# Turning the divided sums behind the product of v, and their product with Wo behind the next slot's sums of v

## The chip, the cores and the metric

The kernel runs on one core of a Trainium2 chip. The metric is the device time of one execution in microseconds; times of different runs are compared by their median. A core has five engines that run side by side, each with its own queue of instructions: TensorE (PE: products and turnings, that is transposes through the array), VectorE (DVE), ScalarE (ACT), GpSimd (POOL), and SyncE (SP), which here issues the transfers. Products land in PSUM, from which DVE or ACT copy them.

## The reference

The input x has 8 sequences of 512 rows of 128 numbers. Two residual blocks follow each other. The first is an attention with 16 heads of width 8, whose weights come from four Newton steps in place of a softmax (here called the stieltjes part):

```python
for _ in range(num_iter):                      # 4
    d = jnp.maximum(lam[..., None] - s, EPS)
    w = jnp.where(mask, d ** (-q), 0.0)
    f = w.sum(-1) - 1.0
    ...
    lam = lam - f / fp
```

The second is a stack of 6 layers, each a windowed attention (16 heads of width 64, windows of 32 rows, each looking at itself and the window before) and a feed forward with a gated gelu, both added to x:

```python
for i in range(DEPTH):                         # 6
    x = attn_layer(shift_tokens(x), Wqkv[i], q_scale[i], k_scale[i], Wo[i]) + x
    x = ffn_layer(shift_tokens(x), ln_g[i], ln_b[i], W1[i], b1[i], W2[i], b2[i]) + x
```

In `attn_layer`, `out = local_attention(q, k, v)` is divided by the softmax's sums, laid side by side over the heads, and `out @ Wo` is the layer's result. The change is about these last steps: divide, turn, multiply with Wo.

## The kernel before

**Units and slots.** The layers run on the sequences as 48 units, one for each layer and sequence. The sequences go in three groups, (0, 1), (2, 3, 4) and (5, 6, 7), and within a group all sequences take a layer before any takes the next. A unit has 16 heads, in 8 pairs; two pairs are a quarter, and one pair is the work of one slot. The main loop runs over `t`, one slot at a time (384 pairs and a few slots more), as a pipeline written out by hand: in slot t it works on pair t, on pair t - 2 and on pair t - 3, and prepares a later quarter.

**The steps of a slot, in the order in which the code issues them.** The names of the tiles are those of the profile.
- `turn` (L733, L738): q and k of pair t are turned on PE into `ptq` and copied by ACT to `qT`, twice.
- `gather` (L787, L795, L796), for pair t - 3: the sums of v, 64 small products into `po`; DVE takes the reciprocal `rs` of the row sums and writes the divided sums `o`.
- `turn_weights` (L776, L777), for pair t - 2: the softmax weights are turned into `pT` and copied by ACT to `prT`.
- `prepare_qk` (L667 and on), for half of a later quarter: two products `m`; DVE multiplies them with tables (`qr`, L672), ACT squares them (`sq`, L678), POOL adds (L682); then sums of squares and scales (L689 to L695). It ends in a call of `gelus`.
- `exponentials` (L769), for pair t - 1, and `gelus`, which runs a waiting gelu between two loads of ACT's tables (L822, L824). `follow` and `marks` keep these ACT instructions in their order.
- `turn_sums` (L804, L808), for pair t - 3: the divided sums `o` are turned on PE into `po` (L804), and ACT copies them to `oT`.
- `weigh` (L752, L757 to L763), for pair t: 64 small products `s`; DVE adds the mask, takes the maximum, POOL subtracts it.
- `prepare_v` (L704, L707): the product `pv`, which ACT copies to `v`; every other slot `spread` then issues the transfers that lay v out by windows.
- `leave` (L812), for pair t - 3: the product of `oT` with Wo, added up over the 8 pairs of a unit in the PSUM tile `acc`. Behind a unit's last pair the sum is added to the sequence's `xT` (L1034), and a feed forward is appended to `parts`.

**The feed forward** is a generator in seven stages (shifted copy, turning `px`, scales, turning `pn`, product `gp` with the gelu's input, product `ap`, product `y`). `further` takes one stage on. It is called once a slot, and three times more in `dense` slots, those that finish pairs of group (0, 1).

**The stieltjes part** is a generator too. `tick(n)` stands between the steps of a slot and advances it by as many of its own steps as the plan for this slot asks. The first two sequences run it alone; for the others it runs beside the layers, and in the last third of the span it is done.

**Order and buffers.** A scheduler puts the instructions of each engine in an order, which follows the order of issue where its own model of the times lets it; on the chip each engine keeps that order. Most PSUM tiles come from one pool of five banks (`bank`, tag "mm": `ptq`, `pT`, `m`, `pv`, the turned sums, the feed forward's and the stieltjes part's). `s` and the sums of v share one buffer (tag "two"), and `acc` has one of its own. The tiles `o2` and `oT2` have one buffer each.

Of the kernel before, what the change touches and what calls it, by code (L numbers as in the profile page):

```python
# [9 lines left out]
F32 = mybir.dt.float32  # L10
BF16 = mybir.dt.bfloat16
AF = mybir.ActivationFunctionType
ALU = mybir.AluOpType
# [3 lines left out]
P = 128  # L17
N = 512
# [32 lines left out]
def tile_kernel(  # L51
# [18 lines left out]
    nc = tc.nc  # L70
# [18 lines left out]
    units = [(l, b) for grp in groups_of for l in range(DEPTH) for b in grp]  # L89
# [10 lines left out]
    ps_c = ctx.enter_context(tc.tile_pool(name="ps_c", bufs=1, space=PSUM))  # L100
# [398 lines left out]
    def bank(shape, name):  # L499
        return ps_a.tile(shape, F32, name=name, tag="mm")  # L500
# [3 lines left out]
    xT = {}  # L504
# [12 lines left out]
    def advance(upto):  # L517
        nonlocal done_steps
        while done_steps < upto:
            next(first, None)  # L520
            done_steps += 1
# [92 lines left out]
    def load_wo(l, hv):  # L614
        wo = wp.tile([P, NPAIR // 2, D], F32, name="wo", tag=f"wo{hv}")
        nc.sync.dma_start(wo, f_wo[l][hv * HC : (hv + 1) * HC, :].rearrange("(c p) d -> p c d", p=P))
        return wo

    def load_tables(l, h):
        tab = wp.tile([P, 2, 4, DHL], F32, name="tab", tag=f"tab{h}")  # L620
        nc.sync.dma_start(tab, tabs[l][:, 2 * h : 2 * h + 2])
        return tab

    def load_ffn_weights(l):
        w1 = wp.tile([P, 2 * DI], F32, name="w1")
        nc.sync.dma_start(w1, f_w1[l])
        w2 = wp.tile([P, NCH, D], F32, name="w2")
        for k, (c0, cn) in enumerate(CH):
            nc.sync.dma_start(w2[:cn, k, :], f_w2[l][c0 : c0 + cn, :])
        return w1, w2  # L630
# [11 lines left out]
    PQ = 2  # L642
# [84 lines left out]
    def turn(a):  # L727
        g, p = a["g"], a["p"]
        a["qT"] = qT = []
        for t in range(2):  # L730
            pt = bank([P, N], "ptq")
            for c in range(NT):
                nc.tensor.transpose(  # L733
                    pt[:, c * P : (c + 1) * P],
                    g["qn"][:, c, t, 2 * p : 2 * p + 2, :].rearrange("p h e -> p (h e)"), ident,
                )
            q = tp.tile([P, N], F32, name=f"qT{t}")
            nc.scalar.copy(q, pt)  # L738
            qT.append(q)
# [31 lines left out]
    def turn_weights(a):  # L771
        pr = a["pr"]
        a["prT"] = prT = tp.tile([P, NT, P], F32, name="prT")
        pT = bank([P, NT, P], "pT2")
        for c in range(NT):
            nc.tensor.transpose(pT[:, c, :], pr[:, c].rearrange("p e k -> p (e k)"), ident)  # L776
        nc.scalar.copy(prT, pT)  # L777

    def gather(a):
        g, p, prT = a["g"], a["p"], a["prT"]  # L780
        po = ps_b.tile([P, 2, N], F32, name="po2", tag="two")
        po = po[:, :, 0 : NT * (DHL + 1)].rearrange("p e (c f) -> p e c f", c=NT)
        for n in range(NQ):
            c, u = n // UB, n % UB
            for e in range(2):
                rows = slice(e * KB, (e + 1) * KB)
                nc.tensor.matmul(  # L787
                    po[u * QB : (u + 1) * QB, e, c, :],
                    lhsT=prT[rows, c, u * QB : (u + 1) * QB],
                    rhs=g["v3"][rows, n, p, :],  # L790
                    start=True, stop=True,
                )
        a["o"] = o = tp.tile([P, NT, 2, DHL], F32, name="o2")
        rs = tp.tile([P, 2, NT], F32, name="rs", bufs=2)
        nc.vector.reciprocal(rs, po[:, :, :, DHL])  # L795
        nc.vector.tensor_tensor(  # L796
            o.rearrange("p c e f -> p e c f"), po[:, :, :, 0:DHL],
            rs.unsqueeze(3).to_broadcast([P, 2, NT, DHL]), ALU.mult,
        )

    def turn_sums(a):
        pt = bank([P, N], "po3")
        for c in range(NT):
            nc.tensor.transpose(  # L804
                pt[:, c * P : (c + 1) * P], a["o"][:, c].rearrange("p e f -> p (e f)"), ident
            )
        a["oT"] = oT = tp.tile([P, N], F32, name="oT2")
        nc.scalar.copy(oT, pt)  # L808

    def leave(a, wo, acc):  # L810
        pp = a["g"]["qt"] * PQ + a["p"]
        nc.tensor.matmul(  # L812
            acc, lhsT=wo[:, pp % (NPAIR // 2), :], rhs=a["oT"],
            start=(pp == 0), stop=(pp == NPAIR - 1),
        )
# [84 lines left out]
    LAG = 2  # L900
    NS = NPAIR
# [3 lines left out]
    wo = {hv: load_wo(l0, hv) for hv in range(2)}  # L905
    tab = [load_tables(l0, h) for h in range(2)]
    w12 = [load_ffn_weights(l0)]
# [19 lines left out]
    def tick(n):  # L927
        if entering:
            next(entering[0], None)
        advance(span[0] + (span[1] - span[0]) * n // TICKS)  # L930

    def further():
        parts[:] = [n for n in parts if next(n, n) is not n]

    def open_quarter(i):
        u, qt = quarters[i]
        if qt == 0 and units[u][0] == 0:
            settle()
        groups.append(begin(u, qt, shifted(units[u][1], ep) if qt == 0 else groups[-1]["xs"]))

    def prepared(g):
        u, qt = g["u"], g["qt"]
        spread(g)
        if u + 1 < len(units) and units[u + 1][0] != units[u][0]:
            if qt % 2:
                wq[qt // 2] = load_qkv(units[u + 1][0], qt // 2)
# [6 lines left out]
        prepare_qk(groups[0], wq[0], tab[h], cs)  # L953
        prepare_v(groups[0], wq[0], cs)
    prepared(groups[0])
    pairs, parts, acc = [], [], None
    slots = len(quarters) * PQ
    end = slots - 3 * NS * DEPTH - NS
    stages = [(0, 5 * STEPS, end, total)]
    if len(groups_of) > 1:  # L960
        n = len(groups_of[0]) * NS * DEPTH + (len(groups_of[1]) - 1) * NS - 8
        g = ready_at[groups_of[1][-1]]
        stages = [(0, 5 * STEPS, n, g), (n, g, end, total)]
    t = -1
    while t < slots + LAG + 1 or parts:
        i, p = t // PQ, t % PQ
        a = done = last = ahead = None
        if 0 <= i < len(quarters):
            a = dict(g=groups[i], p=p)
            pairs.append(a)  # L970
        if LAG <= t < len(pairs) + LAG:
            done = pairs[t - LAG]
        if LAG + 1 <= t < len(pairs) + LAG + 1:
            last = pairs[t - LAG - 1]
        dense = last and units[last["g"]["u"]][1] in groups_of[0] and len(groups_of) > 1
        n0, g0, n1, g1 = next(s for s in stages if t + 2 <= s[2] or s is stages[-1])
        goal = g0 + (g1 - g0) * (t + 2 - n0) // (n1 - n0)
        span[:] = done_steps, max(done_steps, min(goal, total))
        if a:
            turn(a)  # L980
        tick(1)
        if last:
            gather(last)
        tick(2)
        if done:
            turn_weights(done)
        tick(3)

        i, h = (t + 1) // PQ + 1, (t + 1) % PQ
        if i < len(quarters):  # L990
            if h == 0:
                open_quarter(i)
            ahead = groups[i]
            cs = (2 * h, 2 * h + 1)
            prepare_qk(ahead, wq[ahead["qt"] // 2], tab[h], cs)
            u = ahead["u"] + 1
            if ahead["qt"] == NS // PQ - 1 and u < len(units) and units[u][0] != units[u - 1][0]:
                tab[h] = load_tables(units[u][0], h)
        tick(6)
        if dense:  # L1000
            further()
        if 1 <= t < len(pairs) + (0 if a else 1):
            exponentials(pairs[t - 1])
        gelus()
        tick(7)
        if last:
            turn_sums(last)
        if dense:
            further()
        tick(8)  # L1010
        if a:
            weigh(a)
        tick(9)
        if dense:
            further()
        if ahead:
            prepare_v(ahead, wq[ahead["qt"] // 2], cs)
            if h == PQ - 1:
                prepared(ahead)
        tick(10)  # L1020
        further()
        tick(11)
        if last:
            u, qt = last["g"]["u"], last["g"]["qt"]
            l, b = units[u]
            hv = qt // 2
            if last["p"] == 0 and qt == 0:
                acc = ps_c.tile([P, N], F32, name="acc")
            leave(last, wo[hv], acc)
            if last["p"] == PQ - 1:  # L1030
                if qt % 2 and u + 1 < len(units) and units[u + 1][0] != l:
                    wo[hv] = load_wo(units[u + 1][0], hv)
                if qt == NS // PQ - 1:
                    nc.vector.tensor_tensor(xT[b], xT[b], acc, ALU.add)  # L1034
                    parts.append(feed_forward(u, *w12[0]))
        tick(12)
        t += 1
        u = (t + 6) // NS
        if u < len(units):
            need(units[u][1])  # L1040
# [51 lines left out]
```

## Time and profile before

| | |
|---|---|
| median of 3 runs | 4685.11 us (4684.45 to 4686.75) |
| the profiled execution, its time | 4683.56 us |
| its span, first to last instruction | 4681.8 us |
| PE busy | 4029.8 us (86%) |
| DVE busy | 3935.3 us (84%) |
| ACT busy | 3532.1 us (75%) |
| POOL busy | 3177.3 us (68%) |
| mean granted clock of PE | 0.939 |
| L812, product with Wo | 768 instructions, 414.6 us busy |
| L667, products m | 1536 instructions, 759.4 us busy |

Busy time is the time in which the engine worked on an instruction; matmuls overlap, and their ends are modelled, so PE's own pace is better seen from the starts of its instructions. A product in 32-bit floats shows as two instructions. A line of waits names who waited, for whom, for how long in total, how often, and the longest. In a timeline the columns are the start, the time taken, the engine, the line, the operation and its tiles, and, in brackets, the idle time of the engine ahead of it with what ended it.

### The profile page before, as it was taken

To read this page: it belongs to the slowest core of one execution; us is meant where nothing else is said; L and a number is where in the kernel's file an instruction comes from. 1 tells how busy PE (TensorE), PEld (TensorE's weight loads), DVE (VectorE), ACT (ScalarE), POOL (GpSimd) and SP (SyncE) were. 2 spreads that over 40 slices of the span, in tenths; PEclk is the share of its full clock that TensorE was granted. 3 is DMA by queue.
4 is the path that set the end of the run, shared out by engine and by line. 5 is a ranking of instruction groups with operands and counts; after the bars stand their busy time and mean duration, and the time that the engine had idled before them with its cause. 6 is when DMAs were issued, how large, how long until landed. Compare 5 with 4: busy or idle time off the path is not lost.

```text
span 4681.8 us, 165984 instructions
## 1 busy us (share of the span) xinstructions
PE 4029.8 (86%) x68749; PEld 2507.4 (54%) x68749; DVE 3935.3 (84%) x8788; ACT 3532.1 (75%) x6716; POOL 3177.3 (68%) x4081
## 2 busy tenths in 40 slices
PE   4344688887888888898988999998999999999998
PEld 1233455554455544555555555555666666666665
DVE  7878788887888888998998999999787788877785
ACT  7998677777788777888887888888666666666664
POOL 4543666666666666776777767777787777777774
PEclk7667799999999999999999999999999999999999
DMA  1000222222122222232222222222243333333332
GB/s 49 1 1 1 67 59 51 62 55 59 46 66 61 60 53 62 62 72 50 59 67 54 69 54 70 53 59 68 66 102 83 85 90 75 88 79 86 89 75 59
DMA packets 558912, 288.87 MB, mean 62 GB/s; under 512 B 97580, under 2 KB 541264, under 8 KB 558160
## 3 DMA queue, kind: packets, MB, share of 16 engines
q1 hardware_dynamic: 558160, 278.26, 25.4%
q8 instruction: 543, 8.90, 0.8%
q14 instruction: 209, 1.71, 0.1%
HBM read 66.21 MB, written 7.34 MB: 16 GB/s over the span
## 4 chain that ended last, share of the span: by engine, by line
PE 41%; ACT 26%; DVE 22%; POOL 8%; issue 2%; DMA 1%; SPq 1%; ACTq 0%; POOLq 0%; DVEq 0%
PE m L667 8%; ACT d L301 7%; ACT d L309 5%; PE ptq L733 4%; PE pv L704 4%; DVE stw L289 4%; PE acc L812 4%; DVE qr L672 4%; PE po L787 3%; PE s L752 3%; PE pT L776 3%; POOL ns L276 3%; DVE raw L689 3%; ACT sq L678 2%; PE s L263 2%
## 5 line engine op out<-in xcount | busy, mean ns | idle before, releaser
L682 POOL TENSOR_TENSOR qn<-qr 128x512 f32<-128x512 f32 x768 | 970.0, 1280 | 493.6 <-DVE qr L672 440.5
L672 DVE TENSOR_TENSOR qr<-m,tab 128x1024 f32<-128x1024 f32 x768 | 913.5, 1217 | 157.7 <-PE m L667 116.2
L695 POOL TENSOR_TENSOR qn<-qn,ss 128x512 f32<-128x512 f32 x768 | 786.3, 1046 | 299.5 <-ACT ss L692 285.2
L667 PE MATMUL m<-wqkv,xs 128*128 128x512 f32 x1536 | 759.4, 608 | 16.1 <-ACT prT L777 3.7
L678 ACT ACTIVATE sq<-m 128x512 f32<-128x512 f32 x768 | 459.5, 600 | 394.1 <-DVE qr L672 385.1
L301 ACT ACTIVATE d<-ns,lam 128x416 f32<-128x416 f32 (+7 forms) x1024 | 590.4, 625 | 91.6 <-DVE lam L345 71.0
L289 DVE BATCH_NORM_STATS2 stw<-d 128x6 f32<-128x480 f32 (+7 forms) x1024 | 545.8, 563 | 122.7 <-ACT d L309 120.3
L276 POOL TENSOR_TENSOR df<-ns,lam 128x160 f32<-128x160 f32 (+7 forms) x1024 | 400.3, 429 | 307.2 <-DVE sw L343 135.6
L763 POOL TENSOR_TENSOR pr<-pr,nm 128x512 f32<-128x512 f32 x384 | 401.2, 1045 | 253.2 <-DVE ss L690 146.2
L738 ACT COPY qT<-ptq 128x512 f32<-128x512 f32 x768 | 425.0, 586 | 184.5 <-PE ptq L733 183.4
L689 DVE TENSOR_REDUCE raw<-sq 128x16 f32<-128x1024 f32 x384 | 466.6, 1215 | 64.5 <-ACT sq L678 53.2
L733 PEld LDWEIGHTS ptq<-ident,qn 128*128 128x128 f32 x3072 | 364.7, 144 | 207.9 <-issue 110.4
L733 PE MATMUL ptq<-ident,qn 128*128 128x128 f32 x3072 | 428.2, 281 | 34.3 <-POOL qn L695 20.3
L812 PE MATMUL acc<-oT,wo 128*128 128x512 f32 x768 | 414.6, 622 | 39.0 <-ACT oT L808 38.1
L704 PE MATMUL pv<-wqkv,xs 128*128 128x256 f32 x1536 | 440.3, 410 | 7.7 <-ACT sq L678 5.8
L309 ACT ACTIVATE d<-d 128x864 f32<-128x864 f32 (+3 forms) x512 | 441.2, 871 | 0.0
L364 PE MATMUL dTp<-ident,ns 128*128 128x128 f32 x1280 | 231.3, 302 | 184.1 <-POOL ns L276 119.1
L667 PEld LDWEIGHTS m<-wqkv,xs 128*128 128x128 f32 x1536 | 259.8, 194 | 206.6 <-issue 136.6
L787 PE MATMUL po<-v,prT 64*32 64x65 f32 x24576 | 348.5, 226 | 20.3 <-DVE pr L757 19.7
L752 PE MATMUL s<-qT,qT 64*32 64x64 f32 x24576 | 355.8, 226 | 6.0 <-ACT qT L738 5.0
L787 PEld LDWEIGHTS po<-v,prT 64*32 64x32 f32 x24576 | 278.5, 106 | 129.8 <-issue 52.8
L263 PE MATMUL s<-kn,qj 32*32 32x288 f32 (+14 forms) x4096 | 321.2, 419 | 23.0 <-DVE mn L267 17.6
(137 smaller groups left out, 7984.3 us busy)
## 6 DMA issues: line engine op xcount, KB each, us to landing
v<-v SPq DMA_DIRECT2D x2304, 65.0 KB
v<-v SPq DMA_DIRECT2D x768, 48.8 KB
wqkv<-in_L_ffn_Wqkv_dram SPq DMA_DIRECT2D x72, 256.0 KB
v<-v SPq DMA_DIRECT2D x384, 32.5 KB
wqkv<-in_L_ffn_Wqkv_dram SPq DMA_DIRECT2D x72, 128.0 KB
wo<-in_L_ffn_Wo_dram SPq DMA_DIRECT2D x36, 256.0 KB
tab<-tabs SPq DMA_DIRECT2D x36, 256.0 KB
w<-in_L_ffn_W_dram SPq DMA_DIRECT2D x18, 341.0 KB
```

Of the source, the lines that this page charges most:

```text
L289: nc.vector.bn_stats(t["st"][:, 4 * rb + a].rearrange("p u k -> p (u k)"), pieces(d, rb)[a])
L301: nc.scalar.activation(pieces(d, rb)[a], pieces(t["ns"][rb], rb)[a], AF.Ln, bias=t["lam"][:, c : c + 1],)
L309: nc.scalar.activation(e, e, AF.Exp, scale=-1.0)
L667: nc.tensor.matmul(m.rearrange("p t h e -> p t (h e)"), lhsT=xs[:, c * P : (c + 1) * P], rhs=wqkv[:, 0:2, q0 : q0 + HQ * DHL], start=True, ...
L672: nc.vector.tensor_tensor(qr, m.unsqueeze(1).to_broadcast([P, 2, 2, HQ, DHL]), tab[:, i].rearrange("p (k t) e -> p k t e", k=2).unsqueeze( ...
L682: nc.gpsimd.tensor_tensor(g["qn"][:, c].rearrange("p t h (u e) -> p (t h) u e", u=2), halves_of[:, 0], halves_of[:, 1, :, ::-1, :], ALU.add,)
L689: nc.vector.tensor_reduce(raw[:, :, :, 0], sq, axis=AX.X, op=ALU.add)
L695: nc.gpsimd.tensor_tensor(qc, qc, ss[:, i, :].unsqueeze(2).to_broadcast([P, 2 * HQ, DHL]), ALU.mult)
L704: nc.tensor.matmul(pv[:, i], lhsT=xs[:, c * P : (c + 1) * P], rhs=cols, start=True, stop=True,)
L733: nc.tensor.transpose(pt[:, c * P : (c + 1) * P], g["qn"][:, c, t, 2 * p : 2 * p + 2, :].rearrange("p h e -> p (h e)"), ident,)
L787: nc.tensor.matmul(po[u * QB : (u + 1) * QB, e, c, :], lhsT=prT[rows, c, u * QB : (u + 1) * QB], rhs=g["v3"][rows, n, p, :], start=True, s ...
L812: nc.tensor.matmul(acc, lhsT=wo[:, pp % (NPAIR // 2), :], rhs=a["oT"], start=(pp == 0), stop=(pp == NPAIR - 1),)
```

## The change

`turn_sums` moves from ahead of `weigh` to behind `prepare_v`. `leave`, with what hangs on it (the load of the next Wo, the adding into `xT`, the start of a feed forward), moves from the end of the slot to the next slot, behind `gather`; a new name, `owed`, keeps the pair until then. No step is added or left out.

```diff
-    pairs, parts, acc = [], [], None
+    pairs, parts, acc, owed = [], [], None, None
...
-    while t < slots + LAG + 1 or parts:
+    while t < slots + LAG + 1 or parts or owed:
...
         if last:
             gather(last)
+        if owed:
+            u, qt = owed["g"]["u"], owed["g"]["qt"]
+            l, b = units[u]
+            hv = qt // 2
+            if owed["p"] == 0 and qt == 0:
+                acc = ps_c.tile([P, N], F32, name="acc")
+            leave(owed, wo[hv], acc)
+            if owed["p"] == PQ - 1:
+                if qt % 2 and u + 1 < len(units) and units[u + 1][0] != l:
+                    wo[hv] = load_wo(units[u + 1][0], hv)
+                if qt == NS // PQ - 1:
+                    nc.vector.tensor_tensor(xT[b], xT[b], acc, ALU.add)
+                    parts.append(feed_forward(u, *w12[0]))
         tick(2)
...
         tick(7)
-        if last:
-            turn_sums(last)
         if dense:
             further()
...
         tick(10)
+        if last:
+            turn_sums(last)
+        tick(11)
         further()
-        tick(11)
-        if last:
-            u, qt = last["g"]["u"], last["g"]["qt"]
...
-            leave(last, wo[hv], acc)
...
+        owed = last
         tick(12)
         t += 1
```

More of the change, by code (lines that the diff above doesn't have):

```diff
@@ L1020, in tile_kernel @@
         tick(10)
+        if last:
+            turn_sums(last)
+        tick(11)
         further()
-        tick(11)
-        if last:
-            u, qt = last["g"]["u"], last["g"]["qt"]
[L1025 to L1028, printed above, removed]
-            leave(last, wo[hv], acc)
[L1030 to L1035, printed above, removed]
+        owed = last
         tick(12)
```

## The prediction

> **What bounds the kernel now.** I read the slices of the span first, then the busy time by stretch, then what TensorE waits for, and last one slot of the late stretch instruction by instruction.
>
> ```profile
> PE   4344688887888888898988999998999999999998
> ...
> 560.00:1500.00 940.00, 794.77 (x12934) 476.04 (x12926) 803.84 (x1904) 736.72 (x1382) 614.27 (x823) 0.94 0.24 56
> 1500.00:3150.00 1650.00, 1480.44 (x25013) 889.66 (x25005) 1481.84 (x3425) 1334.33 (x2542) 1166.16 (x1519) 0.97 0.26 61
> 3150.00:4640.00 1490.00, 1466.46 (x27864) 976.40 (x27861) 1193.95 (x1930) 978.10 (x1989) 1120.61 (x1154) 1.00 0.36 82
> ```
>
> The first line is PE's busy share in 40 slices; the columns of the others are length, then busy time of PE, PE's weight loads, DVE, ACT and POOL, and the granted clock. The first L812 starts at 567.1 us, so the change hardly reaches what lies before. From 560 to 3150 us (the middle, 206 slots) PE is busy 85% and then 90%, DVE 86% and 90%: two engines near their limit that also wait for each other. From 3150 us (the end, 174 slots) PE is busy 98% at the full clock: PE bounds it, and whatever holds PE there is paid in full.
>
> ```profile
> PE po L804 <- DVE o L796: 39.1, 40, 3.4
> PE acc L812 <- ACT oT L808: 38.1, 47, 1.9
> ...
> PE po L787 <- DVE pr L757: 19.7, 20, 3.2
> ```
>
> These are us in total, times, longest. The first two are what the change touches: the turning (L804) waits for the divided sums, and the Wo product (L812) for the copy oT. By stretch, the groups of costliest lines give L812 33.6 us of idle ahead of it in the middle and 5.0 in the end; L804 has 55.4 and 10.3.
>
> **The change on PE.** No instruction is added or dropped; two steps move. Per slot, PE's main order was ptq, po (L787), pT, m, L804, s, pv, [feed forward], L812. The order of the changed program's instructions shows ptq, po, L812, pT, m, s, pv, L804, [feed forward]; L812 stands right behind po in 307 of 384 slots, so the change does what it says. What a step costs PE depends on its follower, so I took the time from the first start of each step to that of the next, slot by slot in the end (medians):
> - before: ptq to po 0.967, po to pT 0.792, pT to m 0.493, m to L804 1.719, L804 to s 0.530, s to pv 0.787, pv to L812 0.967, L812 to ptq 0.858: 7.11 us.
> - after, from the same neighbours where the trace has them: ptq to po 0.967, po to a full-width product 0.791, L812 to a turning 0.858, pT to m 0.493, m to s 1.812 (one case, and 14 of half the length at 0.954 against 0.860), s to pv 0.787, pv to a turning 0.866 to 0.967, and then four turnings ahead of ptq's 0.436: 7.01 to 7.11 us.
> So the new order costs PE itself nothing; 0.10 us less in 174 slots would be 17 us, but 0.967 is the commoner case of pv, and I take 0.
>
> **The waits it removes.** s and the sums of v share one PSUM buffer, so s also needs the divided sums o. From po, L804 began 0.792 + 0.493 + 1.719 = 3.00 us later; s now begins 0.791 + 0.858 + 0.493 + 1.812 = 3.95 us later. Shortening each wait of L804 by 0.95 us leaves 18.7 of the 55.4 us in the middle and 2.3 of about 10.2 in the end, now at s: credits of 36.7 and 7.9. The waits of L812 as they stand go too: 33.6 and 5.0. Credits: 70.3 in the middle, 12.9 in the end.
>
> **The wait it adds.** ACT takes its instructions in order. oT used to run between the two squares (L678), in time that ACT spent waiting for DVE's qr; in the changed order it stands behind both squares, the exponentials and the copy of v (L707), and ahead of qT. One slot of the end, the one with the gelu:
>
> ```profile
> 3526.76 0.60 ACT L678 ACTIVATE sq<-m 128x512 f32<-128x512 f32 x1
> 3527.38 1.28 ACT L822 ACT_TABLE_LOAD   x1
> 3528.67 1.48 ACT L822 ACTIVATE gate<-gate 128x1536 f32<-128x1536 f32 x1
> 3530.17 1.28 ACT L824 ACT_TABLE_LOAD   x1
> ...
> 3531.59 0.61 ACT L769 ACTIVATE pr<-pr 128x512 f32<-128x512 f32 x1
> ...
> 3532.22 0.56 ACT L707 COPY v<-pv 128x512 f32<-128x512 f32 x1
> 3532.68 1.07 ACT L738 COPY qT<-ptq 128x512 f32<-128x512 f32 x2
> ...
> 3527.24 2.74 PE L872 MATMUL ap<-xn_ffn,w 128*128 128x512 f32 x6
> 3529.82 1.02 PE L812 MATMUL acc<-oT,wo 128*128 128x512 f32 x2
> 3530.68 1.04 PE L733 MATMUL ptq<-ident,qn 128*128 128x128 f32 x8
> 3531.64 0.89 PE L787 MATMUL po<-v,prT 64*32 64x65 f32 x64
> 3532.46 0.66 PE L776 MATMUL pT<-ident,pr 128*128 128x128 f32 x4
> 3532.95 1.88 PE L667 MATMUL m<-wqkv,xs 128*128 128x512 f32 x4
> ```
>
> The second square can't start earlier (its qr ends where it starts), so the ACT chain stays: copy of v at 3532.22. oT would start at 3532.68, where qT starts now, and take the 0.58 us of its row: 3533.26. Where L812 waits in this trace it starts 0.05 us after oT's end, and the next step follows 0.96 us later instead of 0.86, its weight load no longer covered: 3534.27. In this slot the changed order has three of pT's four blocks ahead of L812; one remains, 0.17 us: m at 3534.44 instead of 3532.95. That is 1.49 us. There are 21 such slots in the end: 31.3 us, with nothing behind to make it up, since PE has no idle time. Queued behind the waiting L812 are pT, m, s and pv; qT and prT shift by 0.5 us behind oT, but s needs qT only at 3534.44 + 1.81, so they cost nothing.
>
> On the tables, this slot's rows have each switch at 1.28 us, and the gelu starts 1.29 us after its load did. The Trainium skill (ScalarE: Activation LUTs, What ACT_TABLE_LOAD costs) puts a switch to another set at about 2.66 us, a drain of about 1.38 us included. By that, two switches would push oT 2.7 us further and the 21 slots would cost 89 us; the rows show no such drain, and I go by them.
>
> In a slot without feed forward, the copy of v starts 4.54 us after m and oT would end 5.64 us after m; L812 can start 5.76 us after m. It just fits, and a lost cover of the weight load costs about 0.03 us: 66 slots, 2 us. In slots with px, pn, gp or y, PE has 0.44 to 2.58 us more to do, and nothing waits.
>
> PE's weight loads are busy 976 of 1490 us in the end. The Trainium skill (Perfetto Trace Analysis, Identifying the Most-Contended Engine) judges TensorE's headroom by that share, not by matmul time. By it a third of the end would be free and the 31.3 us could be absorbed, which would make the end 0; but the steps follow one another with no gap, so I keep 31.3.
>
> A second tightening: from m to the next po was 5.83 us and is now 4.97, while DVE needs qr, qr and pr (L757) in between. Laid over the trace of before (end of pr against start of po less 0.86 us), at most 2.8 us in the end and 46.4 in the middle become new waits.
>
> End: 31.3 + 2.0 + 1.4 (half of 2.8) - 12.9 = +22 us.
>
> **The middle** can't be read so sharply, because the scheduler weaves other work between. I bound it: for each slot, end of the copy of v plus 0.58 us, against the end of the next slot's sums of v less 0.86. The lateness adds up to 107 us from 560 to 1500 us and 54 from 1500 to 3150; with the 22 and 24 of pr, 129 and 78 are the upper ends, 0 the lower ones. PE idles 15% and 10% there, and so some of it falls into idle time: I take a third of the first and half of the second, 43 + 39 = 82, less the credit of 70: +12 us.
>
> **Elsewhere.** The adding into xT (L1034) and the start of a feed forward move into the next slot but ahead of its first stage, so the stages stay in their slots. L1034 waits for L812 on DVE, with qr behind it; L812 ends about where o does and m comes 1.35 us later, which covers its 0.68 us. The load of wo moves half a slot on SP; it is used four slots later (28 us), and SP's order is else the same but for a few loads that change places. After 4640 us the chain is serial and has the same steps: 0.
>
> **Sum.** The profiled execution took 4683.56 us (span 4681.8), 1.55 under the median of the runs. 4683.56 + 22 + 12 = 4718, or about 4719 beside the median.
>
> **Rivals.**
> - *Faster*: the middle's waits go and nothing replaces them. For it: L812 and L804 are two of PE's larger waits. Against it: oT sits behind four ACT instructions more. 4685 + 22 - 70 = 4637 us. It decides if new waits in the middle stay under 70 - 22 - 9 = 39 us. Chance 0.15.
> - *No change*: the gelu slots' stall comes, and the middle gives back 13 to 31 us. 4685 us. Chance 0.12.
> - *Much slower*: oT behind the copy of v holds PE through the whole middle. For it: v's copy is late against po, by that overlay, in 41 of the 70 slots from 560 to 1500 us. With two thirds or all of the 207 us on the path: 22 + 138 - 70 = +90 to 22 + 207 - 70 = +159, 4775 to 4844 us. Chance 0.18.
> - The forecast, 4695 to 4775 us: 0.55.
>
> **Numbers.** 0.2% is 9.4 us, about what a measurement of this kernel can tell from none. Faster 0.15, same 0.12, slower 0.73. The range reaches down into the faster case and up to where the much slower one begins: 4672 to 4775.
>
> **What would show it.** In the profile after: in the end, L812 waiting for oT about 1.4 us once per eight slots and L804 waiting for nothing; ACT's idle before the second square longer by oT's 0.5 us; slots without feed forward still near 7.1 us; the end longer by 20 to 30 us. In the middle, L804's wait for o gone, and L812's wait for oT at 40 to 120 us. I am wrong if the stall in gelu slots is missing (oT ahead of the table loads), or if the middle moves by over 60 us either way.

## The result and the profile after

The changed kernel takes 4738.94 us (median of 4 runs, 4735.94 to 4744.94) against 4684.78 us (4682.3 to 4686.75) before: a ratio of 1.0115, 95% interval 1.0103 to 1.0127. That is 54 us slower. The profiled execution took 4735.94 us, its span 4734.2 us. The forecast was 4719, in a range of 4672 to 4775.

The slices, and the busy time by stretch, in the columns of before (length, then PE, weight loads, DVE, ACT, POOL, and the clock):

```profile
PE   4345688887888888998989998998999999999998
...
560.00:1500.00 940.00, 785.33 (x12624) 477.22 (x12623) 768.42 (x1856) 720.57 (x1347) 599.83 (x805) 0.92 0.24 55
1500.00:3150.00 1650.00, 1475.32 (x24955) 886.11 (x24952) 1485.68 (x3418) 1330.91 (x2541) 1166.13 (x1519) 0.98 0.26 60
3150.00:4640.00 1490.00, 1454.56 (x27074) 939.10 (x27073) 1175.83 (x1919) 961.68 (x1957) 1103.72 (x1141) 1.00 0.35 80
```

From 560 to 1500 us every engine does less than before in the same time: work was lost there. From 1500 to 3150 us the rows are nearly those of before. In the end PE has issued 790 matmuls fewer (27074 against 27864) in the same 1490 us and is busy nearly as long, so some of that busy time is time in which it is held: the same 23803 matmuls of the last 151 slots show 1249.6 us busy before and 1269.3 us after.

PE's waits over the whole span:

```profile
PE px L833 <- POOL xs L637: 32.5, 7, 11.2
PE po L787 <- DVE pr L757: 24.6, 28, 2.4
PE acc L812 <- ACT oT L808: 24.0, 33, 2.3
...
PE ptq L733 <- DVE gate L875: 19.8, 23, 2.1
```

L804's waits for o (39.1 us before) are gone from the longer rows; s has 10.0 us of them. L812 still waits for oT, 24.0 us instead of 38.1. Two rows have grown: px for POOL's shifted copy (15.8 us before), and ptq, the turning of q, for DVE's gate (4 times and 6.0 us before): 19 of its 23 waits are in the end, one in each slot with a gelu.

To see where the time goes I lay the traces over each other by the starts of the 384 groups of four m, one to a slot. The difference to before, in us, at four of them and at the end:

| group | time before | changed | dense old | gelu early | both | product alone |
|---|---|---|---|---|---|---|
| 48 | 1138 | +4.2 | -3.8 | +8.0 | -3.7 | -8.8 |
| 72 | 1465 | +21.7 | -2.3 | +21.9 | -3.9 | -8.4 |
| 232 | 3359 | +24.5 | +9.1 | +24.0 | -1.7 | -0.6 |
| 383 | 4612 | +56.1 | +39.7 | +42.8 | +19.6 | +20.6 |
| end of span | 4682 | +52.4 | +36.1 | +39.3 | +16.3 | +16.0 |

(The last four columns are experiments below.) The changed kernel loses 4.2 us up to group 48, 17.5 us between groups 48 and 72, 2.8 us from there to 232 and 31.6 us in the end, and gains 3.7 us in the tail.

**The end.** The same starts give the length of a slot by what else PE does in it (median, us; the last 151 slots):

| | no feed forward | px | gp | ap (the gelu) | y |
|---|---|---|---|---|---|
| before | 7.114 | 7.554 | 9.690 | 9.690 | 9.691 |
| changed | 7.161 | 7.599 | 9.738 | 11.149 | 9.742 |

Slots of every kind are 0.047 us longer, and those with a gelu 1.46 us: 19 of 1.46 and 132 of 0.047 make 34, of which 31.6 are seen. One gelu slot, first ACT, then PE:

```profile
3554.29 0.60 ACT L678 ACTIVATE sq<-m 128x512 f32<-128x512 f32 x1 [0.53 <-DVE qr L672]
...
3559.74 0.56 ACT L707 COPY v<-pv 128x512 f32<-128x512 f32 x1
3560.21 0.58 ACT L808 COPY oT<-po 128x512 f32<-128x512 f32 x1
3560.68 1.08 ACT L738 COPY qT<-ptq 128x512 f32<-128x512 f32 x2
```

```profile
3554.77 2.74 PE L872 MATMUL ap<-xn_ffn,w 128*128 128x512 f32 x6
3557.45 0.42 PE L787 MATMUL po<-v,prT 64*32 64x65 f32 x20
3558.52 0.66 PE L733 MATMUL ptq<-ident,qn 128*128 128x128 f32 x4 [0.66 <-DVE gate L875]
...
3560.34 0.55 PE L776 MATMUL pT<-ident,pr 128*128 128x128 f32 x3
3560.84 1.12 PE L812 MATMUL acc<-oT,wo 128*128 128x512 f32 x2
3561.81 0.27 PE L776 MATMUL pT<-ident,pr 128*128 128x128 f32 x1
3561.91 1.45 PE L667 MATMUL m<-wqkv,xs 128*128 128x512 f32 x3
```

oT ends at 3560.79 and L812 starts at 3560.84, the 0.05 us that a product shows when it waits for oT. m starts 7.14 us after ap; before it was 5.71 (3527.24 to 3532.95). But PE has also stood still ahead of that, 0.66 us at ptq, for a PSUM bank that DVE frees only once the gelu is through. Both hold the slot, and the trace alone doesn't tell what each is worth.

**Groups 48 to 72.** POOL at the end of a unit of the dense slots, before:

```profile
1209.16 1.08 POOL L763 TENSOR_TENSOR pr<-pr,nm 128x512 f32<-128x512 f32 x1
1210.33 0.60 POOL L635 COPY xs<-xT 64x512 f32<-64x512 f32 x1
1210.99 0.61 POOL L637 COPY xs<-xT 64x511 f32<-64x511 f32 x1
1211.87 3.71 POOL L276 TENSOR_TENSOR ns<-ns,lam 128x416 f32<-128x416 f32 x4 [0.27 <-DVE lam L282]
```

and the same place after, then PE's next step there:

```profile
1210.36 1.05 POOL L763 TENSOR_TENSOR pr<-pr,nm 128x512 f32<-128x512 f32 x1
1212.10 3.71 POOL L276 TENSOR_TENSOR ns<-ns,lam 128x416 f32<-128x416 f32 x4 [0.69 <-DVE lam L282]
...
1227.13 0.60 POOL L635 COPY xs<-xT 64x512 f32<-64x512 f32 x1
1227.79 0.61 POOL L637 COPY xs<-xT 64x511 f32<-64x511 f32 x1
```

```profile
1228.46 1.12 PE L833 MATMUL px<-ident,xs 128*128 128x128 f32 x4 [11.04 <-POOL xs L637]
```

The adding into xT started at 1209.59 before and starts at 1212.62 now, 3 us later. POOL's shifted copy, the first step of the feed forward, was ahead of the stieltjes part's adds to ns and now stands behind 15 us of them and the two steps woven in. PE waits 11 us for it, and the two slots from group 54 take 54.8 instead of 44.6 us. (The kernel before has such a place too, one unit earlier: there px waits 10.3 us at 1105.9 us.)

That is 10.2 of the 17.5 us. Another 9.9 go in the three slots from group 61, at the next unit's end, where the copy follows the adding at once (1335.59 and 1336.34 us); the other slots give some back. What waits there, from 1321.7 to 1380.4 us:

```profile
DVE qr L672 <- PE m L667: 12.5, 1, 12.5
PE pn L853 <- POOL xt L846: 9.2, 4, 8.3
```

Before, in the same three slots, the first was 0.5 us and the second 5.9 us. PE's granted clock is lower there as well (0.83 against 0.90; 0.75 against 0.81 in the two slots from group 54). No run here tells whether that is a cause or follows from the longer waits.

### The profile page after: what moved, and what is told of

It is laid out like the page before. It is cut to its first block, busy times and chain, and to the rows that moved or that the text cites. A ratio compares the mean times of both kernels' runs of the same rounds, so it can differ in the third digit from the quotient of the medians.

```text
span 4734.2 us, 165897 instructions
## 1 busy us (share of the span) xinstructions
PE 4053.3 (86%) x68749; PEld 2500.7 (53%) x68749; DVE 3925.1 (83%) x8788; ACT 3530.4 (75%) x6716; POOL 3177.2 (67%) x4081
## 4 chain that ended last, share of the span: by engine, by line
PE 41%; ACT 25%; DVE 23%; POOL 7%; issue 3%; SPq 1%; DMA 1%; ACTq 0%; DVEq 0%; POOLq 0%
PE m L667 7%; ACT d L301 7%; PE acc L812 5%; DVE qr L672 5%; ACT d L309 5%; PE ptq L733 5%; PE pv L704 4%; DVE stw L289 4%; PE po L787 4%; PE s L752 3%; DVE raw L689 3%; PE pT L776 2%; POOL ns L276 2%; ACT sq L678 2%; PE y L882 2%
## 5 line engine op out<-in xcount | busy, mean ns | idle before, releaser
L733 PE MATMUL ptq<-ident,qn 128*128 128x128 f32 x3072 | 437.8, 282 | 71.0 <-DVE gate L875 19.8
L812 PE MATMUL acc<-oT,wo 128*128 128x512 f32 x768 | 446.5, 664 | 25.8 <-ACT oT L808 24.0
L733 PEld LDWEIGHTS ptq<-ident,qn 128*128 128x128 f32 x3072 | 353.3, 144 | 159.8 <-issue 43.6
L752 PEld LDWEIGHTS s<-qT,qT 64*32 64x32 f32 x24576 | 274.2, 106 | 261.5 <-issue 185.7
L787 PE MATMUL po<-v,prT 64*32 64x65 f32 x24576 | 364.8, 228 | 27.8 <-DVE pr L757 24.6
L777 ACT COPY prT<-pT 128x512 f32<-128x512 f32 x384 | 225.0, 586 | 178.0 <-PE pT L776 175.7
```

What stands on the lines that cost most here:

```text
L733: nc.tensor.transpose(pt[:, c * P : (c + 1) * P], g["qn"][:, c, t, 2 * p : 2 * p + 2, :].rearrange("p h e -> p (h e)"), ident,)
L787: nc.tensor.matmul(po[u * QB : (u + 1) * QB, e, c, :], lhsT=prT[rows, c, u * QB : (u + 1) * QB], rhs=g["v3"][rows, n, p, :], start=True, s ...
L812: nc.tensor.matmul(acc, lhsT=wo[:, pp % (NPAIR // 2), :], rhs=a["oT"], start=(pp == 0), stop=(pp == NPAIR - 1),)
```

## The experiments

The theories: (1) oT behind the table loads makes the gelu slots' stall; (2) POOL's copy behind its adds makes the loss between groups 48 and 72. Rivals: the place of L812 itself on PE, behind the sums of v, PSUM banks that come free late, and, for (2), the late turning in whatever way. Each figure is a median; the ratio is to runs of the kernel before on the same chip.

**Old order in the dense slots.** In `dense` slots turning and product stand where they stood before.

```diff
         if dense:
+            turn_sums(last)
             further()
...
-        if last:
+        if last and not dense:
             turn_sums(last)
...
+        if last and dense:
...
+            leave(last, wo[hv], acc)
...
-        owed = last
+        owed = None if dense else last
```

> The changed kernel, with the old places of the turning and of the Wo product in the slots of the first group of sequences (the dense ones); all later slots as changed. Theory (POOL's queue): of the 54 us lost, about 20 were lost between 1190 and 1470 us, because the adding into xT came 3 us later and POOL's shifted copy xs, the feed forward's first step, then stood behind 15 us of POOL's adds; with the old order there, these 20 come back: 4719 us. Rival (PE's new order costs a little in every slot of the middle, and it only showed there): the first 1500 us give back a quarter of it at most, 4733 us or more.

4719.91 us, ratio 1.0074 (1.0061 to 1.0087): 19 us back, the number that theory (2) gave. Between groups 48 and 72 it loses 1.5 instead of 17.5 us, and between 1190 and 1480 us px no longer waits. So the loss comes from the new order in the dense slots. The edit puts back the turning and the product together, though, and with them POOL's order; it can't tell these apart. In the later middle it loses 11 us that the changed kernel doesn't lose; of that below.

**Early turning in gelu slots alone.**

```diff
+        early = bool(waiting)
...
+        if last and early:
+            turn_sums(last)
...
-        if last:
+        if last and not early:
             turn_sums(last)
```

> The changed kernel, with the turning back at its old place (ahead of the scores) only in slots in which a gelu waits; the Wo product stays in the next slot everywhere. Theory (oT stands behind the table loads): the 21 slots of the end with a gelu fall from 11.15 to about 9.74 us, 30 us back: 4709 us. Rival (the place of the Wo product on PE, behind the sums of v, is what costs): nothing changes, 4739 us.

4723.29 us, ratio 1.0087 (1.0074 to 1.0101): 16 us back, about half of what theory (1) alone asks. The gelu slots fall from 11.15 to 10.51 us, not to 9.74. PE in one of them:

```profile
3552.60 2.74 PE L872 MATMUL ap<-xn_ffn,w 128*128 128x512 f32 x6
3555.18 0.60 PE L733 MATMUL ptq<-ident,qn 128*128 128x128 f32 x4
3555.71 0.30 PE L787 MATMUL po<-v,prT 64*32 64x65 f32 x2
3556.35 0.66 PE L733 MATMUL ptq<-ident,qn 128*128 128x128 f32 x4 [0.35 <-DVE gate L875]
3556.94 0.88 PE L787 MATMUL po<-v,prT 64*32 64x65 f32 x62
3557.74 1.13 PE L812 MATMUL acc<-oT,wo 128*128 128x512 f32 x2
```

L812 no longer waits. But ptq comes right behind ap, 0.86 us sooner than with L812 ahead of it; its second half meets a bank that is still held until the gate is multiplied, and the scheduler has cut po in two around that. In the old order L812's 0.86 us lay in just that gap. In the changed kernel even the first half of ptq waited. The code's five shared banks fit this: ap takes three, and the product of v and the turned sums hold the other two until ACT has copied them behind the table loads. With oT early one of these is free.

**Both at once.**

> Both at once: the old order in the dense slots, and the early turning in slots with a gelu. If the two places are the whole loss but for 0.05 us in each slot of the end (the weight load of the Wo product, no longer covered: 174 slots, 8 us), and the middle's waits give nothing: 4690 us. If the removed waits of the middle were worth their credit (70 us) and only hidden by the two losses: 4630 to 4660 us. If losses are also elsewhere: above 4700.

4703.23 us, ratio 1.0039 (1.0026 to 1.0051). 36 us of 54 are back, not 49, so the third case holds, losses elsewhere: the gelu slots stay at 10.51 us. At group 232 this kernel is 1.7 us ahead of the one before, so the 70 us of credit that I gave the removed waits are not there.

**The product late, outside the dense slots; the turning where it was.** The edit is `turn_sums(last)` back ahead of `weigh`, and the condition on `dense` of the first experiment.

> Only the Wo product moves into the next slot, and only outside the dense slots; the turning stays at its old place everywhere. Theory (the loss comes from oT's place on ACT and from POOL's queue in the dense slots): neither is touched; what is left is 0.05 us a slot in the end, 8 us, less some of the 34 us that the Wo product waited for oT in the middle: 4670 to 4693 us. Rival (the Wo product behind the sums of v is what costs): 4709 us or more.

4708.57 us, ratio 1.0052 (1.004 to 1.0065). Missed by 16 us or more, and the rival's 4709 is met: with the turning untouched, the late L812 costs 24 us. The gelu slots take 10.51 us, the others 0.047 more than before. In the profiled execution 22 us are lost in the end and 12 between groups 72 and 232, where the run with the product late everywhere (below) loses 8; that stretch scatters from version to version.

**The turning alone.** `turn_sums` behind `prepare_v`; `leave` in its own slot, behind it.

> Only the turning moves behind the product of v; the Wo product is issued in the same slot, at its end, right behind it. The scheduler still puts the Wo product behind the next sums of v in the end, but POOL's shifted copy in the dense slots keeps its old place among POOL's adds. Theory: the gelu slots' stall comes in full and the dense loss doesn't: 4719 us, of which the end loses 31 to 39. Rival (the move of the Wo product is needed for any loss): 4690 us or less.

4829.02 us, ratio 1.0311 (1.0297 to 1.0326): missed by 110 us. I had read the scheduler's order in a gelu slot, where L812 did move behind the sums of v. In slots without feed forward it comes soon after the turning, and waits:

```profile
PE acc L812 <- ACT oT L808: 99.1, 180, 1.9
```

Such a slot takes 7.98 us, 0.86 more than before. So the two halves of the change belong together: moved on its own, the turning leaves L812 too close behind it. Between groups 48 and 72 it loses 19 us as well, although POOL's copy keeps its place there:

```profile
1211.83 0.60 POOL L635 COPY xs<-xT 64x512 f32<-64x512 f32 x1
1212.49 0.61 POOL L637 COPY xs<-xT 64x511 f32<-64x511 f32 x1
1213.28 3.71 POOL L276 TENSOR_TENSOR ns<-ns,lam 128x416 f32<-128x416 f32 x4 [0.17 <-DVE lam L282]
```

The two slots from group 54 lose 3.6 us here, against 10.2 in the changed kernel, and the three from group 61 lose 9.0, with DVE waiting 13.1 us for m. So theory (2) is not shown: POOL's order may explain some 7 us at one unit's end, while the late turning loses as much in all without it. By which way it does so I did not follow up.

**The product alone.** `turn_sums` back at its old place, the rest as changed.

> Only the Wo product moves into the next slot, everywhere; the turning stays at its old place. POOL's shifted copies keep their old places. Theory: no stall in gelu slots (9.74 us), no dense loss, 0.05 us a slot in the end: 4675 to 4693 us. Rival (the move of the Wo product, with the adding into xT behind it, makes the dense loss by itself): about 4710 us.

4703.04 us, ratio 1.0039 (1.0027 to 1.0052). Its rival is out: no loss between groups 48 and 72, so the late product alone costs the dense slots nothing. Measured from the nearest start of a group, the adding into xT is not later than before at group 54 and 1.1 us later at the next two unit ends (1.1 and then 1.9 and 1.8 us in the changed kernel), so this run is no sharp test of a late adding. The theory's 4693 is passed by 10 us, by the gelu slots once more (10.51 us): by group 232 this kernel is level with the one before, and 21 us behind at group 383.

**The product behind m.** The `if owed` part moves behind `prepare_qk`.

> The changed kernel, with the Wo product issued later still: behind the products m of the next slot. oT stays behind the table loads. Theory (in a gelu slot PE waits only because the Wo product needs oT): it is needed 3 us later, so the gelu slots of the end fall from 11.15 to 9.8 us or so, 28 us back in the end. Rival (oT and v hold their PSUM banks until behind the table loads, and the turning of q waits for a bank): the gelu slots keep 0.8 us or more of the 1.46, and the end gets back 14 us at most. In the dense slots the adding into xT comes later still, so the loss before 1500 us stays at 20 us or grows.

4734.15 us, ratio 1.0105 (1.0091 to 1.0118). Gelu slots take 10.28 us. L812 has 3 us more for oT here, so 0.59 us of the 1.46 are not its waiting; the rival named 0.8 or more, so neither figure is met. Slots without feed forward grow to 7.31 us, and the end loses 32 us, as in the changed kernel. Between groups 48 and 72 it loses 20 us, as expected.

**Without the table loads**, in the kernel before and in the changed one. The gelu becomes a plain copy, so this part of the computation is left out.

```diff
-            g = follow(nc.scalar.activation(flat, flat, AF.Gelu), marks["act"])
-            marks["act"] = follow(
-                nc.scalar.preload_act_table_set("natural_log_exp_and_others"), g
-            )
+            marks["act"] = follow(nc.scalar.activation(flat, flat, AF.Identity), marks["act"])
```

> The kernel before with the gelu replaced by a plain copy on ACT, and without the two table loads around it; this part of the computation is left out. In the end PE is the bound and the loads lie beside it, so the end stays as it is; in the middle ACT saves 2.6 us in each of 27 units, and some of it shows: 4660 to 4685 us. It is there to be compared with the next run.

> The changed kernel with the same part left out. Theory (the stall in gelu slots is the two table loads, 2.6 us, ahead of oT): the gelu slots of the end need no more than the other slots with three products (9.74 us), so this one stands 30 us nearer to its counterpart than the changed kernel to the kernel before: some 24 us over it, or less where the dense loss changes too. Rival (the place of the Wo product or of the turning on PE is what costs): still 50 us or more over it.

4672.6 us (ratio 0.9972, 0.9961 to 0.9982) and 4682.3 us (0.9994, 0.9986 to 1.0003). They stand 9.7 us apart, where the changed kernel and the one before stand 54. The gelu slots of the end take 9.691 and 9.750 us: without the table loads the stall is gone, both the wait for oT and the one at the bank. The end then costs 4.9 us between groups 232 and 383, near the 7 that 0.047 us a slot ask for 151 slots. 24 was too high: by group 72 the two stand 17 us apart, as with the loads, but from there to group 232 they come 7 us closer again.

**The product late, but on time in gelu slots**; the turning at its old place. `owed = last` only where no gelu waits, else `leave` at the end of the slot.

> Only the Wo product moves into the next slot, except in slots in which a gelu waits, where it is issued at the end of its own slot as before; the turning stays at its old place. Theory now (with oT early, a gelu slot still takes 10.51 us against 9.69, because the turning of q comes 0.86 us earlier, meets banks that DVE frees only behind the gelu, and the Wo product no longer fills that time): the gelu slots of the end fall to 9.69 to 9.74 us, 15 us less than with the product late everywhere: 4688 us. Rival (the late product costs as much in whatever slot): 4701 us or more.

4689.63 us, ratio 1.0011 (1.0002 to 1.002): as expected within 2 us. Gelu slots fall from 10.51 to 9.80 us, a little short of the 9.74 expected. So most of what L812's place costs, it costs in that slot, and only 0.047 us in the others.

**The product late up to the end, and in the tail.** The same edit with `late = t < end or t >= slots - 2`.

> Only the Wo product moves into the next slot, and only in the middle (up to the slot where the stieltjes part ends) and in the last few slots; in between and for the turning the old order. If the late product gains in the middle as the run with the product alone shows it (9 us) and in the tail (4 us), and its cost lies in the end alone (24 us): 4671 to 4677 us, a little faster than the kernel before. If the gain in the middle is paid back where the two orders meet: 4685 us.

4684.48 us, ratio 0.9998 (0.9989 to 1.0007): no change, the second of the two expected cases. It is 10 us ahead at group 160 and 5.6 at 192, but the lead is 2.4 at group 232 and gone by 383. No version here that does the whole computation beats the kernel before.

## Why the prediction was right, and where it was not

The sign, the place of the largest term and the size of that term held; the sum around it did not. A gelu slot of the end was to grow by 1.49 us: it grew by 1.46, and oT and L812 stand as they were drawn. Pricing the table switch by its rows was right: in the changed kernel, too, the gelu starts 1.29 us after its load. By the Trainium skill's figure (ScalarE: Activation LUTs, What ACT_TABLE_LOAD costs), about 2.66 us a switch, my estimate for the slot would have been 4.2 us, and no row here shows that. PE absorbed none of it, so its weight-load share was no measure of slack here either.

What that term left out is a second cause. I wrote that L812 waits for oT. With oT early the slot gets back 0.64 us (11.15 to 10.51), part of which may be the bank that the turned sums no longer hold; 0.82 us remain, and 0.71 of these go when L812 is back ahead of ptq in that slot (10.51 to 9.80). They are the gap at ptq, whose bank waits for the gelu through DVE. I had the order of these steps, and summed PE's steps as if the banks were free. The two causes overlap in time, so the sum came out right without the second. Without the table loads both are gone.

The steps that failed:
- *L812 to a turning, 0.858 us.* It measured 0.962 (median of the end), without any wait: behind the 64 small products its weight load is not covered (rows in the last section). pT to m fell from 0.493 to 0.437. The slot is 7.16 us, not 7.01 to 7.11: about 8 us over 174 slots where I wrote 0 and 2.
- *The credit of 12.9 us in the end.* At most some 2 us of it are seen: the last 151 slots lose 31.6, where the slot lengths alone ask 34. The sum for the end was 22.
- *The dense slots, where adding and feed forward were put at 0.* The forecast looked at which slot the stages are issued in and at DVE's order around L1034, but not at POOL's queue, and gave the dense slots no term of their own. They cost 17.5 us between groups 48 and 72, and the first experiment gives back 19 us in all. The late turning is needed for it (with the product alone there is no loss) and is enough (moved alone, it loses 19). POOL's copy behind 15 us of adds is seen at one unit's end and is worth some 7 us at most by the difference to that run; the rest of the way from the late turning to the loss stays open.
- *The middle, +12 us (82 of new waits less 70 of credit).* Between groups 72 and 232 the changed kernel loses 2.8 us, and with both places undone 2.2. L804's waits did go. L812's waits for oT from 560 to 3150 us fell from 32.9 to 21.7 us where I had written 40 to 120, so the lateness of the overlay was not there. But the credit did not reach the time either, because other waits took the place of those removed: for the same 29,000 matmuls between these groups PE stands idle 190 us before and 195 after. The largest that grew is ptq behind ACT's squares (11.8 us, 0.9 before), and DVE is as busy there as PE (1695 and 1698 us of 1894 and 1896). Versions that differ only in distant slots scatter by some 10 us in that stretch (the first experiment loses 11, the changed kernel 3); I can't tell a cause for that.
- *After 4640 us, 0.* The tail gains 3.7 us; why, no run here was made to tell.

So the forecast of +34 for +54 has a right core in the gelu slots, 6 us too little for PE's steps, a credit of 13 in the end that did not come, and a middle for which +12 was written out of two wrong terms while +24 came by group 232, most of it in the dense slots in a way that was not priced. That two wrong terms left a number of the right sign there is luck.

## What to carry to other kernels

When a step is moved, price its first consumer on every queue, not only in the slot of the program: here a producer 3 us later put its consumer behind 15 us of other work that stood next in POOL's queue, and PE waited 11 us for it at that place. And a product that seems to cost its own time may be filling a gap: look at what the step behind it needs (here a PSUM bank, freed by DVE behind a gelu behind two table loads) before taking the filler away. And a wait of PE that was removed where DVE is equally busy was worth next to nothing here, since other waits took its place. Last, an experiment that undoes two moves at once shows where a loss lies, but not which move makes it.

## What the runs showed of the hardware

The time from L812's start to its follower's is 0.858 us behind full-width products and 0.962 behind the 64 small ones, with no wait shown. The rows of its weight load (PEld) show why, first before, then after:

```profile
3345.92 0.41 PEld L812 LDWEIGHTS acc<-oT,wo 128*128 128x128 f32 x2
3346.13 1.02 PE L812 MATMUL acc<-oT,wo 128*128 128x512 f32 x2
...
3354.93 0.30 PEld L812 LDWEIGHTS acc<-oT,wo 128*128 128x128 f32 x2
3354.93 1.13 PE L812 MATMUL acc<-oT,wo 128*128 128x512 f32 x2
```

Behind the product of v the load starts 0.21 us ahead of the product, behind the small products together with it. So the order of products has a price of its own, 0.05 us a slot here after what pT gives back. Each table load took 1.28 us and the activation behind it started 1.29 us after the load did, with no drain between.
